# A hybrid attention kernel on one core: the first chunk of a layer, the head of a routing stage and the emptying of some row sums, rearranged

## The chip, the core and the metric

The kernel runs on one core of a Trainium2 chip. A core has a matrix engine (TensorE, PE in the profile; its weight loads are PEld), a vector engine (VectorE, DVE), a scalar engine (ScalarE, ACT), a general engine (GpSimd, POOL) and a sync engine (SyncE, SP) that mostly issues transfers. Every engine works through its own instructions in order and waits on semaphores for the others. The matrix engine writes to PSUM, which is handed out in banks of 128 x 512 values. The metric is the device time of one execution in microseconds (us). All data are float32.

## What is computed

The input is one image of 256 channels and 64 x 64 positions. Layer 0 is a windowed linear attention, layer 1 a softmax attention over all 4096 positions and a mixture of 8 experts, of which each position uses two:

```python
# layer 0: x + attention(groupnorm(x))
q, k = sigmoid(Wq x), sigmoid(Wk x);  v = Wv x / max(|Wv x|, 1e-12)      # 8 heads of 32 channels
for w in (1, 2, 4):                     # boxes of 64 // w around each position
    wk, wkv = box_sum(k), box_sum(outer(k, v))
    outs.append(q . wkv / (q . wk + 1e-6))
x = x + concat(outs) Wout + bout
# layer 1, t is the 4096 x 256 matrix of positions
q, k, v = split(layernorm(t) w_qkv + b_qkv)
t = t + softmax(q k^T / sqrt(256)) v w_out + b_out
xt = layernorm(t);  logits = xt Wr + br;  weights, idx = top2(softmax(logits))
y_e = gelu((layernorm(xt) * ln_g[e] + ln_b[e]) W1[e] + b1[e]) W2[e] + b2[e]   # for the two experts
t = t + sum(weights * y[idx])
```

## The kernel before

The positions are cut into 8 chunks of 512, or 32 tiles of 128. Instructions go into each engine's queue in the order in which the program makes them; a small planner (`behind`, `tick`, `flush`) defers the use of scores by a step or two, and `tc.issue_after` places an instruction behind a named one. There are four stages.

**Layer 0** works on two groups of four heads, one after the other. `prepare` (L309) forms k, v and their sums over cells of 64 positions, then q (`by_channel(0, i)`, L360, sigmoid L367) and, held in the list `later`, four calls that project k by channel. Then it computes the denominators: for each of the three windows it builds differences of running sums (`tall`, L490 to L499, the copy on ScalarE) and products with q (L514), and multiplies them by a small matrix on PE (L517). The calls in `later` are taken one by one after every product part of four rows (L528). `attend` (L590) then computes the attention without expanding the outer products: scores of q and k (L662 for the band's part, L734 for the chunk's), multiplied by masks on VectorE or, after a copy by ScalarE, on GpSimd (`masked`, L548 to L569, where lines 561 and 565 are), and multiplied by v into PSUM (L693, L750). For windows of 32 and 16 positions there are four bands; in each, two banks of row sums are begun from prepared cell sums (L681), filled (L693), and at the band's last step both are emptied by ScalarE into `raw` (L706, two copies per band; 2 windows x 4 bands x 2 groups make 32). Six banks hold scores, two hold sums. The output projection is L638, added to `t` at L642.

**Layer 1, projections** (L808 to L933). A prologue issues the weights' and biases' loads (L821 to L845), turns the bias rows by a PE transpose (L847) into columns (`bqk`, L849), forms the sums of the router's matrix and its product with the output weights (L856 to L882), and only then goes over the 8 chunks. For each chunk: statistics of the *next* chunk (`begin`, L793 to L799, with a square root on ScalarE), the reciprocal of this one's (L802), and for each of its four tiles a normalized tile `hn` on VectorE (L898, in a pool of two buffers), two transposes on PE (L808) and a copy by ScalarE (L809); then 16 products for q and k (L914; evicted by VectorE at L918, with the largest magnitude at L919) and 16 for v with the router's logits (L925; L932, L933).

**Layer 1, attention** (L970 to L1106) is one loop over query chunks, halves of the heads and key tiles. The denominators of a half are turned over through DRAM and applied some steps later, except for the very last one, where `divide` (L1069 to L1073) computes the reciprocal of a 128 x 512 bank at once and multiplies by it. After the loop, the last four tiles are projected (L972), added to `t` (L975), and their statistics taken (L793, L794).

**Routing and experts** (L1180 on). The routing's head loads three sets of the experts' rows, turns them into columns by three PE transposes (L1237 to L1240), stores them to DRAM (L1244), and computes the second normalization (L798 to L802, L1252 on), the logits (L1275 on) and the places of all positions. Then 36 expert steps follow (L1460 to L1496), whose columns are loaded back from DRAM, and the ending (L1537 on) combines the two experts' outputs.

## Time and profile before

| | us |
|---|---|
| median of 3 runs | 2881.29 |
| lowest and highest run | 2879.69, 2881.95 |
| the profiled execution | 2876.29 |
| its span (first to last instruction) | 2874.5 |
| layer 0, from the start to the last L638 | 0 to 1001 |
| layer 1's projections | 1001 to 1120 |
| layer 1's attention | 1120 to 2287 |
| routing, to the first expert product | 2287 to 2340 |
| experts and ending | 2340 to 2874.5 |

The mean clock granted to TensorE over the span is 0.976 of full speed. The profile's page gives busy times per engine, and the trace gives the start and length of every instruction with the idle time of its engine before it and what ended that. Where the releaser is called "issue", the engine waited for nothing that the trace shows. Times inside the execution are given below as the trace has them, in us from the start of the span.

### The profile page before, as it was taken

The page shows a single profiled execution, that of the slowest core. Times are in us where ns is not written, and L with a number is a line of the kernel's source. Part 1 is how long each engine was busy: PE and PEld are TensorE (multiplying, and loading weights), DVE is VectorE, ACT ScalarE, POOL GpSimd, SP SyncE. Part 2 cuts the span into 40 slices and gives each one's busy share as a digit, 9 for nine tenths or more (in the row PEclk, how much of TensorE's full clock was granted, in tenths as well). Part 3 has the DMA queues.
Part 4 walks back from the last instruction along what each step waited for, and adds up shares of the span by engine and source line. Part 5 has one row for each costly group of instructions (what it writes and reads, how often), then busy time and mean ns, then how long its engine had stood idle before and what let it go on. Part 6 is the DMA issues. An engine that isn't in the chain of part 4 may idle for free.

```text
span 2874.5 us, 73093 instructions
## 1 busy us (share of the span) xinstructions
PE 2722.7 (95%) x31182; PEld 1265.9 (44%) x31182; DVE 2078.1 (72%) x3019; ACT 1504.6 (52%) x2086; POOL 717.9 (25%) x804
## 2 busy tenths in 40 slices
PE   6889999988999999999999999999999779999996
PEld 5454346735434553222222222222222258888884
DVE  6758788575778777999999999999999841111113
ACT  3232423223332314888888888888888643222222
POOL 1067778116777621000000000000000022222220
PEclk9999999999999999999999999999999969999997
DMA  5000000000000000000000000000000056666665
GB/s 140 6 26 28 7 31 13 7 7 24 24 14 27 27 1 1 6 6 6 6 5 6 6 6 6 5 6 6 6 6 6 8 193 205 193 220 196 194 220 187
DMA packets 104212, 149.71 MB, mean 52 GB/s; under 512 B 18338, under 2 KB 79368, under 8 KB 103876
## 3 DMA queue, kind: packets, MB, share of 16 engines
q1 hardware_dynamic: 88984, 118.05, 12.7%
q0 software_dynamic: 6528, 17.83, 2.2%
q10 hardware_dynamic: 8364, 9.02, 0.9%
q8 instruction: 249, 4.08, 0.6%
q14 instruction: 87, 0.71, 0.1%
HBM read 126.76 MB, written 18.12 MB: 50 GB/s over the span
## 4 chain that ended last, share of the span: by engine, by line
PE 57%; DMA 2%; DVE 1%; issue 1%; ACT 0%; SPq 0%; POOL 0%; ACTq 0%; DVEq 0%; POOLq 0%
PE ps_two L1025 20%; PE ps_acc L991 18%; PE ps_hp L1485 8%; PE ps_yp L1494 8%; PE ps_den L972 1%; PE ps_den L991 1%; DMA y<-yrows 1%; PE ps_tp L1460 1%; DMA w<-in_L_ffn_W 0%; PE ps_two L972 0%; DVE t L1537 0%; DMA yrows<-y,target 0%; DVE rec L1072 0%; ACT pe L1036 0%; DVE total L1043 0%
## 5 line engine op out<-in xcount | busy, mean ns | idle before, releaser
L1036 ACT ACTIVATE pe<-ps_two 128x1024 f32<-128x1024 f32 x1024 | 992.4, 1021 | 142.5 <-PE ps_two L1025 127.3
L1043 DVE TENSOR_TENSOR total<-total,pe 128x1024 f32<-128x1024 f32 x928 | 1058.0, 1214 | 0.0
L1025 PE MATMUL ps_two<-qk 32*64 32x512 f32 x8192 | 620.2, 613 | 3.6 <-POOLq L978 1.8
L991 PE MATMUL ps_acc<-pe,v 128*32 128x512 f32 x4096 | 546.4, 605 | 0.2 <-ACT pe L1036 0.2
L561 ACT COPY sm<-ps_sc 128x384 f32<-128x384 f32 (+3 forms) x454 | 218.5, 511 | 523.8 <-PE ps_sc L734 344.3
L565 DVE TENSOR_TENSOR sm<-ps_sc,mask 128x512 f32<-128x512 f32 (+3 forms) x740 | 340.0, 519 | 71.8 <-PE ps_sc L734 68.0
L565 POOL TENSOR_TENSOR sm<-sm,mask 128x192 f32<-128x192 f32 (+3 forms) x428 | 350.1, 847 | 111.9 <-ACT sm L561 111.5
L1025 PEld LDWEIGHTS ps_two<-qk 32*64 32x64 f32 x8192 | 166.5, 129 | 421.0 <-PE ps_two L1025 379.0
L1488 ACT ACTIVATE hid<-ps_hp,cols 128x256 f32<-128x256 f32 (+1 forms) x288 | 133.0, 462 | 360.6 <-PE ps_hp L1485 359.5
L1303 POOL MEMSET on<- 128x256 f32 x1 | 0.3, 311 | 1166.6 <-PE ps_den L991 1166.6
L991 PEld LDWEIGHTS ps_acc<-pe,v 128*32 128x32 f32 x4096 | 80.7, 108 | 416.5 <-issue 402.5
L1485 PE MATMUL ps_hp<-xe,w 128*128 128x256 f32 (+1 forms) x1152 | 246.8, 371 | 0.0
L1494 PE MATMUL ps_yp<-w,hid 128*128 128x256 f32 x1088 | 240.8, 379 | 0.0
L734 PE MATMUL ps_sc<-qk 32*64 32x384 f32 (+3 forms) x3584 | 231.9, 458 | 0.0
L1485 PEld LDWEIGHTS ps_hp<-xe,w 128*128 128x128 f32 x1152 | 201.3, 190 | 39.5 <-ACT hid L1488 5.3
L1494 PEld LDWEIGHTS ps_yp<-w,hid 128*128 128x128 f32 x1088 | 204.2, 190 | 26.4
L750 PE MATMUL ps_acc<-sm,v 128*32 128x256 f32 (+3 forms) x2688 | 213.2, 419 | 0.2
L565 POOL TENSOR_TENSOR sm<-sm,ycut 128x384 f32<-128x384 f32 (+4 forms) x146 | 147.5, 1031 | 250.4 <-ACT sm L561 250.1
L1464 DVE TENSOR_SCALAR xe<-ps_tp,cols 128x256 f32<-128x256 f32 (+1 forms) x72 | 34.8, 525 | 239.6 <-PE ps_tp L1460 217.1
L565 DVE TENSOR_TENSOR sm<-ps_sc,ycut 128x384 f32<-128x384 f32 (+4 forms) x254 | 128.8, 559 | 90.0 <-PE ps_sc L662 88.0
L1496 DVE TENSOR_TENSOR y<-ps_yp,b 128x256 f32<-128x256 f32 x68 | 28.9, 424 | 194.8 <-PE ps_yp L1494 194.7
L734 PEld LDWEIGHTS ps_sc<-qk 32*64 32x64 f32 (+1 forms) x3584 | 108.6, 157 | 111.4 <-DVE sm L565 67.6
(237 smaller groups left out, 2230.6 us busy)
## 6 DMA issues: line engine op xcount, KB each, us to landing
w<-in_L_ffn_W SPq DMA_DIRECT2D x72, 1024.0 KB
by<-recs SPq DMA_DIRECT2D x48, 256.0 KB
b<-in_L_ffn_b SPq DMA_DIRECT2D x36, 128.0 KB
rows<-in_x SPq DMA_DIRECT2D x16, 256.0 KB
zrows<-act SPq DMA_DIRECT2D x4, 1024.0 KB
y<-yrows SPq DMA_DIRECT2D x8, 512.0 KB
y<-yrows ACTq DMA_DIRECT2D x8, 512.0 KB
rec<-recs SPq DMA_DIRECT2D x60, 64.0 KB
```

What stands on the lines that cost most here:

```text
L561: nc.scalar.copy(sm[:, :used], sc[:, :used])
L565: done = engine.tensor_mul(to, of, mk.unsqueeze(1).to_broadcast(list(to.shape)))
L734: nc.tensor.matmul(scs[h][u : u + rows, at : at + n], kT[hs[h], P * i + u : P * i + u + rows], qT[hs[h], CH * ix + CELL * c0 : CH * ix + C ...
L750: nc.tensor.matmul(acc[hs[h], CELL * c0 : CELL * c1], v[:, i, hs[h]], sms[h][:, at : at + n], start=not begun[0], stop=last and at == plac ...
L991: nc.tensor.matmul(to[D * hd : D * (hd + 1), :], lhsT(hd), rhs[:, hd, :], start=start, stop=stop, skip_group_check=True,)
L1025: nc.tensor.matmul(sc[hd // 2][CELL * u : CELL * (u + 1), hd % 2, :], qk[hs, 1, g, P * i + CELL * u : P * i + CELL * (u + 1)], qk[hs, 0, g ...
L1036: nc.scalar.activation(pe[:, pair, :], s, AF.Exp, scale=C**-0.5)
L1043: add = nc.vector.tensor_add(to, first[:, pair, :] if i == 1 else to, pe[:, pair, :])
L1464: nc.vector.tensor_scalar(xe[:, k, :n], tp[:, k, :n], cols[:, gain], cols[:, shift], op0=ALU.mult, op1=ALU.add,)
L1485: nc.tensor.matmul(hp[:, :n], w1[:, k, tok(m)], x_now[:, k, :n], start=k == 0, stop=k == KC - 1)
L1488: nc.scalar.activation(hid[:, m, :n], hp[:, :n], AF.Gelu, bias=cols[:, m : m + 1])
L1494: nc.tensor.matmul(yp, hid[:, m, tok(j)], w2[:, m, :], start=m == 0, stop=m == NH - 1)
```

## The change

It has seven parts.

- In layer 1's prologue the bias transposes and the router's products become two functions. Chunk 0's four normalized tiles and their transposes come first; then `biases()` and the statistics of chunk 1; then chunk 0's products; then `router()`, and then chunk 1. `issue_after` places them so on VectorE and on PE.
- The normalized tiles `hn` get four buffers instead of two.
- The experts' columns are turned right after chunk 2's products for v, with the rows loaded on SP and the copies on ScalarE; the store goes to SP too. They leave the routing.
- The last `divide` works in four quarters of 128 columns: reciprocal and product of each.
- The emptying of each band's two banks in layer 0 goes half to ScalarE and half to VectorE.
- The first deferred k projection is made before the denominators' loop starts, so each later one comes one part earlier.
- Square roots of a constant are placed where ScalarE's table of functions is to change: after the last sigmoid of layer 0's second preparation, and at the start of the routing stage.

```diff
+            if g == KC - 1:
+                with tc.issue_after(sigmoid[0]):
+                    nc.scalar.sqrt(root, ident[:, :1])
...
             q = qk[:, 0].rearrange("p (i n) -> p i n", n=CH)
+            later.pop(0)()
             for w, r in enumerate(REACH):
...
-                                    nc.scalar.copy(
+                                    (nc.vector.tensor_copy if u else nc.scalar.copy)(
                                         raw[:, :, q0 : q0 + CELL], accs[u].rearrange("p (i n) -> p i n", n=CELL)
                                     )
...
+    def expert_columns(pool, ps):
+        cols = pool.tile([P, NE, NH + 2 * KC], F32, name="cols")
+        at = 0
+        for name, n in (("L1_ffn_b1", NH), ("L1_ffn_ln_g", KC), ("L1_ffn_ln_b", KC)):
+            rw = pool.tile([NE * n, P], F32, name=f"{name}_rows")
+            nc.sync.dma_start(rw, a[name].rearrange("e (k p) -> (e k) p", p=P))
+            tp = ps.tile([P, CH], F32, tag="mm", name="ps_mm")
+            nc.tensor.transpose(tp[:, : NE * n], rw, ident[: NE * n, : NE * n])
+            nc.scalar.copy(cols[:, :, at : at + n], tp[:, : NE * n].rearrange("p (e k) -> p e k", e=NE))
+            at += n
+        nc.sync.dma_start(crows.rearrange("e p n -> p e n"), cols)
...
+            def biases():
+                tp = ps.tile([P, CH], F32, tag="mm", name="ps_mm")
+                nc.tensor.transpose(tp[:, :6], rows6, ident[:6, :6])
+                nc.vector.tensor_copy(bqk, tp[:, :6])
+
+            def router():
...
             begin(0)
             for c in range(NCH):
-                if c + 1 < NCH:
+                if 0 < c < NCH - 1:
                     begin(c + 1)
                 norm.end(NB * c, NB * (c + 1))
                 for i in range(NB * c, NB * (c + 1)):
-                    hn = work.tile([P, C], F32, name="hn")
-                    nc.vector.tensor_scalar(
+                    hn = work.tile([P, C], F32, name="hn", bufs=4)
+                    last = nc.vector.tensor_scalar(
...
+                if c == 0:
+                    with tc.issue_after(last.ins), tc.issue_after(turned.ins):
+                        biases()
+                        begin(1)
...
+                if c == 0:
+                    with tc.issue_after(biased.ins), tc.issue_after(product.ins):
+                        router()
+                if c == 2:
+                    expert_columns(win, ps)
...
                                     rec = work.tile([P, CH], F32, tag="rec", name="rec")
-                                    nc.vector.reciprocal(rec, den[0])
-                                    times(rec)
+                                    for n in range(CH // P):
+                                        nc.vector.reciprocal(rec[:, tok(n)], den[0][:, tok(n)])
+                                        nc.vector.tensor_mul(to[:, tok(n)], to[:, tok(n)], rec[:, tok(n)])
...
+        root = small.tile([1, 1], F32, name="root")
+        nc.scalar.sqrt(root, ident[:1, :1])
         cst.update(constants_of("m", wts))
...
-            cols = r_work.tile([P, NE, NH + 2 * KC], F32, name="cols", bufs=1)
...
-                nc.scalar.dma_start(rw, a[name].rearrange("e (k p) -> (e k) p", p=P))
...
-            nc.scalar.dma_start(crows.rearrange("e p n -> p e n"), cols)
```

The body of `router()` is the old prologue's, line for line, and is left out here.

## The prediction

> **What bounds the kernel now.** I read the page's first two parts, then the granted clock and the engines in windows of 1 us over the head of layer 1, then the timelines of that head, of a later chunk, and of the end of the attention, and the answer for line 706.

> ```profile
> PE 2722.7 (95%) x31182; PEld 1265.9 (44%) x31182; DVE 2078.1 (72%) x3019; ACT 1504.6 (52%) x2086; POOL 717.9 (25%) x804
> ...
> PEclk9999999999999999999999999999999969999997
> ```

> TensorE (PE) is busy for 95% of 2874.5 us, and its clock drops where it had nothing to do. None of the long loops behind that 95% (L991, L1025, L1485, L1494) changes, so only the gaps between them are in play. By windows (start:end, length, busy share of PE, PEld, DVE, ACT, POOL, then granted clock, DMA share, GB/s):

> ```profile
> 1003.00:1004.00 1.00, 0.00 (x0) 0.00 (x0) 1.00 (x7) 0.62 (x1) 0.00 (x0) 0.57 0.95 332
> ...
> 1019.00:1020.00 1.00, 1.00 (x2) 0.34 (x1) 1.00 (x5) 0.00 (x0) 0.00 (x0) 0.50 0.00 0
> 1020.00:1021.00 1.00, 1.00 (x4) 0.46 (x3) 0.41 (x2) 0.00 (x0) 0.00 (x0) 0.90 0.00 0
> ```

> PE stands still from 1000.6 to 1007.2 and then runs at half clock to about 1020, though its products have been dense since 1014.78. The timeline of that head (start, length, idle before with releaser):

> ```profile
> 1003.38 1.28 ACT L799 ACT_TABLE_LOAD   x1 [8.06 <-DVE ln_mv L794]
> ...
> 1007.26 0.24 PE L847 MATMUL ps_mm<-cst,bias_rows 6*128 6x6 f32 x1 [6.67 <-DMA L_attn_b_out_all<-in_L_attn_b_out]
> ...
> 1007.61 0.17 DVE L849 COPY bqk<-ps_mm 128x6 f32<-128x6 f32 x1 [2.95 <-PE ps_mm L847]
> ```

> PE starts on the bias rows at 1007.26. VectorE (DVE) stands 2.95 us before their eviction, with chunk 0's reciprocal and normalized tiles (first L898 at 1009.50) queued behind it; the first QKV product (L914) comes at 1014.78. A later chunk begins like this:

> ```profile
> 1054.93 0.73 PE L808 MATMUL ps_mm<-cst,hn 128*128 128x128 f32 x4 [0.49 <-DVE hn L898]
> ...
> 1056.13 4.13 PE L914 MATMUL ps_mm<-act,wqkv 128*128 128x512 f32 x9 [0.46 <-ACT act L809]
> ```

> Two short waits per chunk, one for a normalized tile, one for its copy. Who waits for L706's copies in layer 0 (us, times):

> ```profile
>   PEld ps_acc L681: 3.6, 6
>   PEld ps_acc L750: 2.8, 4
> ```

> 6.4 us is all that PE ever waits for them. And the end of the attention with the routing's head:

> ```profile
> 2277.91 3.36 DVE L1072 RECIPROCAL rec<-ps_den 128x512 f32<-128x512 f32 x1 [1.15 <-PE ps_den L991]
> ...
> 2282.11 3.80 PE L972 MATMUL ps_two<-wo,act 128*128 128x264 f32 x10 [2.72 <-DVE act L1067]
> ...
> 2289.93 0.17 DVE L1315 TENSOR_SCALAR steps<-cstm 128x16 f32<-128x16 f32 x1 [2.66 <-issue]
> 2292.52 0.31 DVE L1240 COPY cols<-ps_mm 128x64 f32<-128x64 f32 x2 [2.42 <-issue]
> ```

> Here DVE is the path: one reciprocal of 3.36 us holds PE, and 2.42 us pass ahead of the column copy that nothing in the profile explains, though PE had its input ready at 2288.2.

> **The change, part by part.** All of it is against the profiled execution, 2876.29 us.

> *Chunk 0 ahead of the router.* The new order on PE is transposes, bias transpose, chunk 0's products, its V products, and then the router's small products among chunk 1's transposes. On DVE, chunk 0's four tiles come before the bias eviction. With the root table loaded earlier (1.28 us off ACT's path), the tiles are made at about 1004 to 1006 and turned before the weights are in. The DMA share falls to 0.22 in 1006 to 1007 and the bias rows release PE at 1007.26. Adding their transpose, 0.24, the first product starts at 1007.5; it stands behind that landing on PE as the router did. The sixteen products took 1014.78 to 1024.43 = 9.65 with the first 5.3 us at half clock; I take the same, as in both orders they follow an idle stretch and small work: 1017.15. V products took 1024.43 to 1027.99 = 3.56: 1020.7. Router products were at half clock 1.02 + 1.00 + 1.09 + 0.60 + 1.07 = 4.8, so 2.4 at full: 1023.1. Their two evictions (0.43 each) stand between products: 0.8, 1023.9. Chunk 1's transposes took 1027.99 to 1030.42 = 2.43: 1026.3; the waits within them, 0.49 and 0.60, now hold router products: about 1025.3. Before, it was 1030.42. I take **-5.0**. Ends: the router at half clock throughout costs 2.4 more (-2.6); a start at 1006.9 and evictions fully covered gain 1.4 more (-6.5). Behind the moved bias eviction on DVE stand chunk 1's statistics (8 instructions, about 2.3 us) and then the evictions of chunk 0, whose first came 3.8 us after its products began, so they are covered; uncovered they would cost what DVE lacks, under 1 us.

> The row is that the clock was still 0.50 in 1019 to 1020, 5.3 us after dense products began and 12.7 after the first small one. [...]

> *Four normalized tiles instead of the pool's default.* At the six later boundaries the 0.49 goes; what is late next is ACT, whose copy (0.70 for two) holds L914 by 0.46 already. I take 0.35 x 6 = **-2.1**, ends 0 (ACT was as late) and -2.9 (6 x 0.49).

> *Expert columns in chunk 2.* Three transposes of 0.23 to 0.28 us each (rows L1239), with three copies by ACT: 0.75, and 0.25 for a bank that waits: **+1.0**, ends 0.4 (at full clock, no wait) and 2 (three waits of an ACT copy, 0.4, added). The transposes' rows are loaded some 40 us earlier. Those three loads join SP behind the weights, 0.37 to 0.46 each to issue; nothing is due on SP behind them, nor behind the column store, until 2274. Four DMA issues leave ACT's queue at the routing (0.53, 0.60, 0.33, 0.42), where ACT waited anyway.

> *Divide in quarters.* The reciprocal of 128x128 is 0.94 (row L620), a product of that size 0.29 (row L1319); in eight steps 4 x 1.23 = 4.9, less some 0.06 overlap per step: done at 2282.5 instead of 2282.05. But the first two quarters are done by 2280.3, and the last product's rows no longer come after ten products in a row (3.80, the clock going to 0.50). DVE's tail work from there is 2282.86 to 2287.27 = 4.41, of which 1.06 was waiting for PE; without it 2282.5 + 3.35 = 2285.9: **-1.35**, ends -0.5 (half of the 1.06 stays, the start as now) and -2.2.

> *Routing's head.* With no column copies the normalization's add (2292.75) stands directly behind L1315's step (2289.93). The two copies are 0.23; the 2.42 is either a code fetch behind a branch (the instruction queue's packets land at 2290.5 and 2293.0) or something the copies waited for. Either way the copies' place is gone, and the instructions behind the branch have shifted by eight. I take it as gone: **-2.65**, ends -0.2 (the gap stays, at the next instruction) and -2.8. The whole chain to the first expert product (2339.5) hangs on this DVE work, so it passes through. ACT's table load at 2288.51 had been hidden already: 0. What is late next is ACT's own chain (L1261, 15.8 us, ending 2312.26), which ends level with DVE's first piece but starts from the same root, so it moves too.

> *L706 split.* Sixteen of 32 copies, 0.589 each, leave ACT (9.4 us, at places where ACT waits) and come to DVE at 0.69 (the 128x512 copy, row L340). PE waits for the first copy of a pair, which stays. Behind DVE's copy stand the next step's masks. At 161.81 DVE is idle for 2.02 us, at 296.0 for 2.78, so 0.69 lies in that: **0**, ends -2 (a third of the 6.4) and +6.

> *k ahead of denominators.* The same PE instructions from 88.6 to 124.6; DVE's waits there (4.49 and 3.40) change places with them, and the long denominators to 138.87 are the same: **0**, ends -1 and +1. The square root's table load lands in layer 0's last preparation, where ACT waits 1.31 ahead of a copy at 612.82 needed at 617.94: 0.

> Sum: -5.0 - 2.1 + 1.0 - 1.35 - 2.65 = **-10.1**, so 2866.2 profiled. The median of the runs, 2881.29, stands 5.0 above the profiled execution; with that, **2871**.

> **The rivals.**
> *The head gives half (chance 0.2).* The 2.42 shows up again at the next instruction, and the router runs at half clock: 2.4 + 2.4 less. Net -5.3, time 2876. For it: PE's clock in this region took 13 us to rise, and the gap carries no releaser. Against it: the router now follows 13 us of dense products.

> *The copies on DVE hold the masks (chance 0.1), slower.* DVE works in order; if its copy waits for the sums as ACT did (5.7 us over 7 cases, 0.36 per copy) with the next masks behind, PE waits for their banks: 16 x (0.69 + 0.36) = +16.8, net +6.7, time 2888. It needs over 0.63 us of PE time per copy, so nearly all of it uncovered. For it: PE waits 67.6 us for DVE's masks at L734. Against it: idle times of 2 to 2.8 us at the places looked at, and 71.8 us of DVE waiting for PE before its masks.

> *The change does only the rest (inside the first).* If the tiles' order gave nothing at the later chunks and the columns cost 2 us, the sum would be -7.0: 2874.3.

> **How the numbers follow.** My forecast, 2871, has 0.7 with its own range of 2865 to 2876; the half gain 0.2; the slower case 0.1. 0.2% is 5.8 us, about what a measurement of this kernel can tell from no change: under 2875.5 is faster, over 2887.1 slower. Faster: 0.62 of the 0.7 and 0.08 of the half gain, 0.70. Slower: 0.08 of the 0.1. Same: the rest, 0.22. All best ends together give -17.0 (2864.3), all worst +5.7 (2887.0); the range goes 1 us of the runs' spread below the first, and ends at 2881, where the two faster cases and their bounds end, leaving out the slower one: 2863 to 2881.

> **What would show it.** The first QKV product at 1007 to 1008 and chunk 1's near 1025.4, with the clock at 1.00 by about 1013; later chunks 12.5 us apart, that of the columns a little longer; the last row statistic at about 2285.9 on the old scale; less than 1 us between L1315's step and the normalization's add; layer 0's end where it was, within 2 us. It would be wrong if layer 0 ends over 5 us later, if a new idle row of PE names the masks behind a DVE copy, or if the 2.4 us comes back as issue time on DVE.

## The result, and the profile after

The changed kernel took 2866.28 us (median of 6 runs, 2862.69 to 2871.48) against 2880.08 us (6 runs, 2879.19 to 2881.95): a ratio of 0.9951, 95% interval 0.9938 to 0.9964. Two further measurements on other chips gave 0.9956 (0.9942 to 0.9969) and 0.9955 (0.9941 to 0.9968). So it is faster, by 13 to 14 us where 10 were forecast, and 2866.3 lies just inside the forecast's own range (2865 to 2876).

The page after:

```profile
PE 2719.1 (95%) x31182; PEld 1264.0 (44%) x31182; DVE 2088.4 (73%) x3038; ACT 1497.5 (52%) x2075; POOL 717.9 (25%) x804
...
PEclk9999999999999999999999999999999979999997
```

ACT has lost 7 us and DVE gained 10, mostly the sixteen copies that changed hands; the long loops are the same. The page shows nothing of where the time went, so I cut the span into stages at the same instructions in every trace. Three executions of the changed program were profiled (two of them among the experiments below); each row begins where the one above it ends:

| stage, us | before | changed | again | third |
|---|---|---|---|---|
| layer 0, to the last L638 (after: L641) | 1000.59 | 1005.34 | 1000.67 | 999.61 |
| head: to the first product of chunk 1 | 29.83 | 23.28 | 23.34 | 23.47 |
| chunks 1 to 7 | 87.68 | 84.97 | 85.00 | 84.97 |
| to the last denominators of the attention | 1159.77 | 1159.71 | 1159.78 | 1159.70 |
| last divide, projection, statistics | 9.24 | 7.06 | 7.06 | 7.05 |
| branch to the normalization's add | 5.65 | 2.91 | 3.00 | 3.01 |
| rest of the routing | 46.78 | 47.48 | 47.09 | 46.91 |
| experts | 489.56 | 489.17 | 489.48 | 489.68 |
| ending | 45.41 | 44.62 | 44.51 | 44.67 |
| span | 2874.50 | 2864.56 | 2859.93 | 2859.10 |

The first two spans differ by 9.9 us, almost the forecast's 10.1, but that agreement is an accident: layer 0 happened to take 4.75 us longer in the first profile of the changed kernel, which the other two do not repeat, and the stages from layer 1 on gave 14.7.

The head, in the timeline after:

```profile
1008.05 0.20 ACT L807 ACTIVATE ln_rstd<-ln_rstd 128x4 f32<-128x4 f32 x1 [7.99 <-DVE ln_rstd L806]
...
1009.09 1.94 PE L816 MATMUL ps_mm<-cst,hn 128*128 128x128 f32 x8 [3.75 <-issue]
...
1011.86 0.24 PE L877 MATMUL ps_mm<-cst,bias_rows 6*128 6x6 f32 x1 [0.83 <-DMA bias_rows<-in_L_attn_b_qkv]
...
1012.03 8.91 PE L947 MATMUL ps_mm<-act,wqkv 128*128 128x512 f32 x16
```

No table load stands ahead of the square root, the transposes are done when the bias rows land, and the products follow at once: 6.7 us after layer 0 instead of 14.2. The granted clock is the column behind POOL's (1.00 is full speed). In steps of 3.4 us, the kernel before and then the changed one:

```profile
1010.00:1013.40 3.40, 3.31 (x16) 2.74 (x14) 2.00 (x6) 0.68 (x2) 2.17 (x3) 0.50 0.00 0
1013.40:1016.80 3.40, 2.76 (x6) 1.28 (x6) 2.82 (x14) 1.01 (x4) 2.24 (x3) 0.50 0.00 0
1016.80:1020.20 3.40, 3.40 (x6) 1.33 (x5) 1.60 (x5) 0.00 (x0) 0.00 (x0) 0.50 0.00 0
1020.20:1023.60 3.40, 3.40 (x10) 1.49 (x9) 2.62 (x8) 0.20 (x1) 0.00 (x0) 1.00 0.00 0
```

```profile
1008.80:1012.20 3.40, 2.28 (x10) 1.90 (x11) 2.76 (x11) 1.49 (x4) 0.00 (x0) 0.50 0.73 249
1012.20:1015.60 3.40, 3.40 (x4) 1.34 (x5) 3.40 (x16) 0.20 (x1) 3.11 (x5) 0.50 0.02 5
1015.60:1019.00 3.40, 3.40 (x9) 1.54 (x8) 3.40 (x6) 0.21 (x1) 2.67 (x4) 0.99 0.00 0
```

Before, a step with PE busy for 3.31 us of router products and transposes (1010.0 to 1013.4) was followed by two more at half clock, and the clock rose behind the first step that the 128x512 products filled (1016.8 to 1020.2). After, the first step of that kind (1012.2 to 1015.6) came at once.

A later chunk's start, after:

```profile
1039.16 1.28 PE L816 MATMUL ps_mm<-cst,hn 128*128 128x128 f32 x8
...
1040.90 7.13 PE L947 MATMUL ps_mm<-act,wqkv 128*128 128x512 f32 x16 [0.46 <-ACT act L817]
```

All eight transposes run without a wait for a tile; PE's wait for ScalarE's copy is 0.46 us, as before.

The end of the attention and the routing's head, after:

```profile
2273.39 1.77 DVE L1111 RECIPROCAL rec<-ps_den 128x128 f32<-128x128 f32 x2 [1.18 <-PE ps_den L1029]
...
2277.38 1.70 PE L1010 MATMUL ps_two<-wo,act 128*128 128x264 f32 x6 [0.86 <-DVE act L1112]
...
2283.21 0.18 DVE L1342 TENSOR_SCALAR steps<-cstm 128x16 f32<-128x16 f32 x1 [2.67 <-issue]
2283.29 0.17 DVE L806 TENSOR_SCALAR ln_rstd<-ln_mv 128x32 f32<-128x32 f32 x1
```

PE waits 0.5 and 0.9 us for quarters of the divide where it waited 2.72 for all of it, and the 2.42 us behind the first instruction of the routing are gone.

### The profile page after: what moved, and what is told of

It reads as the page before. It is cut to its first block, busy times and chain, and to the rows that moved or that the text cites. A ratio compares the mean times of both kernels' runs of the same rounds, so it can differ in the third digit from the quotient of the medians.

```text
span 2864.6 us, 73084 instructions
## 1 busy us (share of the span) xinstructions
PE 2719.1 (95%) x31182; PEld 1264.0 (44%) x31182; DVE 2088.4 (73%) x3038; ACT 1497.5 (52%) x2075; POOL 717.9 (25%) x804
```

## The experiments

The theory to test: the head, the buffers, the divide and the place behind the branch give the gain, each in its stage; layer 0 gives nothing. The rivals: the 2.42 us were a wait of the column copies; router products warm the clock as well as any; layer 0's 4.75 us belong to the change. Some kernels ran once, and are read by their stages; a single time is given, but it can't tell 2 us from nothing here.

**Three parts undone in one kernel**, each in a stage of its own.

```diff
-                                    (nc.vector.tensor_copy if u else nc.scalar.copy)(
+                                    nc.scalar.copy(
...
-                    hn = work.tile([P, C], F32, name="hn", bufs=4)
+                    hn = work.tile([P, C], F32, name="hn")
...
+                                    nc.vector.reciprocal(rec, den[0])
+                                    nc.vector.tensor_mul(to, to, rec)
```

> The changed kernel with three parts undone that lie in different stages: both copies of a band on ScalarE, two buffers for the normalized tiles, the last divide at once. Read by stage against the changed kernel. Chunks: my account is that each of the six later boundaries gets 0.55 us longer (3.3 in all); if the buffers were not what shortened them, 0. Divide: the last statistics come 2.2 us later after the end of the attention. Bands: between -1 and +1 us for all of layer 0. Routing's head: vector-engine code is the same there as in the changed kernel, with no column copies, but the first instruction behind the branch stands eight places earlier, where it stood in the kernel before. If the 2.42 us was code loading, it comes back between the first instruction and the next (over 2 us); if it was a wait of the column copies, the next instruction follows within 0.2 us. Time with code loading about 2874, without about 2872.

Four of the six later boundaries went from 12.27 back to 12.82 us, one from 12.27 to 12.93, and the one with the columns from 12.93 to 13.43; the divide's stage from 7.06 to 9.06. Layer 0 ended at 997.7, sooner than in any profile of the changed kernel, so no loss by the copies on ScalarE is seen. And the gap came back, at the same distance behind the branch, though no column copy stands there:

```profile
2282.59 0.18 DVE L1341 TENSOR_SCALAR steps<-cstm 128x16 f32<-128x16 f32 x1 [2.93 <-issue]
2282.67 0.18 DVE L806 TENSOR_SCALAR ln_rstd<-ln_mv 128x32 f32<-128x32 f32 x1
...
2285.11 0.42 DVE L1301 TENSOR_TENSOR logit<-ln_mv,wr_sum 128x256 f32<-128x256 f32 x1 [2.27 <-issue]
```

Two instructions run, then 2.27 us pass. In the kernel before two had run as well, the step at 2289.93 and a wait. A packet of 8 KB of the instruction queue starts at 2280.8, the next at 2283.4; each is followed by instructions 1.7 to 1.8 us later. One time: 2868.76, against 2872.97 for the kernel before on the same chip.

**The columns back in the routing's head**, copied by VectorE as before, all else as changed.

```diff
-                if c == 2:
-                    expert_columns(win, ps)
...
+            cols = r_work.tile([P, NE, NH + 2 * KC], F32, name="cols", bufs=1)
...
+                nc.vector.tensor_copy(
```

> The changed kernel with the experts' columns back in the routing's head, as before (row loads on ScalarE's queue, copies on VectorE), and out of chunk 2. Chunk 2 to 3 gets about 0.65 us shorter. In the routing's head the code-loading theory expects the copies to cost 0.3 us and no gap over 1 us ahead of them, as the first instruction behind the branch is six places later than in the kernel before: net about -0.3 us. The rival, a wait of these copies, expects the 2.4 us ahead of them again: net about +2.1 us.

```profile
2282.51 0.17 DVE L1353 TENSOR_SCALAR steps<-cstm 128x16 f32<-128x16 f32 x1 [2.67 <-issue]
2282.93 0.31 DVE L1278 COPY cols<-ps_mm 128x64 f32<-128x64 f32 x2 [0.25 <-issue]
2283.15 0.17 DVE L806 TENSOR_SCALAR ln_rstd<-ln_mv 128x32 f32<-128x32 f32 x1
```

The copies are there and the gap is not: the first instruction lies six places behind where it lay before. They cost 0.57 us between the first instruction and the add, rather than 0.3. Chunk 2 to chunk 3 fell from 12.93 to 12.28. One time: 2866.0.

**Eight more tiny instructions in the kernel before.**

```diff
+                spare8 = work.tile([P, 1], F32, name="spare8")
+                for _ in range(8):
+                    nc.vector.memset(spare8, 0.0)
```

> The kernel before with eight more tiny fills of one scratch column on VectorE at the start of layer 1's attention, nothing else changed; the column copies stay in the routing's head. Code loading: the first instruction behind the branch moves by eight places, and the 2.42 us ahead of the column copies falls under 0.5 us; routing ends 2.4 us earlier. A wait of the copies: the 2.42 us stays as it is. The fills themselves lie beside PE's attention: 0.

```profile
2288.14 0.18 DVE L1318 TENSOR_SCALAR steps<-cstm 128x16 f32<-128x16 f32 x1 [2.67 <-issue]
2288.53 0.31 DVE L1243 COPY cols<-ps_mm 128x64 f32<-128x64 f32 x2 [0.22 <-issue]
```

From the first instruction to the add 0.62 us instead of 2.82. VectorE's records ahead of the branch's target are 4570 in the trace of the kernel before and 4569 with three parts undone, the two with the gap; they are 4578 here, 4577 in the changed kernel and 4576 with the columns back, and none of these has it (counts to within a record or two). With the two runs above this settles that the 2.42 us were no wait of the copies: the gap goes with the place of the branch's target. That it is code loaded in pieces, and that the target's place in a piece decides, is my reading; the trace doesn't show which packet holds which instruction. In the changed kernel, too, a second packet starts 2.4 us behind the first (2281.4 and 2283.8), but no gap follows there. The column copies were only the next instructions there. One time: 2872.84, no better than the 2872.97 of the kernel before: in its profile the attention took 1.5 us longer, with a step at half clock at its start.

**The router ahead of chunk 0's products again.**

```diff
                         biases()
+                        router()
                         begin(1)
...
-                if c == 0:
-                    with tc.issue_after(biased.ins), tc.issue_after(product.ins):
-                        router()
```

> The changed kernel with the router's small products put back ahead of chunk 0's products (behind its transposes and the bias transpose), all else as changed. If small products and transposes do not raise the clock: they run at half clock, 4.8 us and their evictions; the clock rises one or two steps of 3.4 us after the dense products begin, as in the changed kernel; chunk 1 then starts 2.5 to 3.5 us later than in the changed kernel. The rival, that any work on PE warms the clock: it is up when chunk 0 begins, the sixteen products take 7 instead of 8.75 us, and chunk 1 starts within 1 us of where it does in the changed kernel.

Head to chunk 1: 25.49 us, 2.0 to 2.2 more than as changed, just under my 2.5. One time: 2868.15. The clock was at 0.50 from 1007.6 to 1017.8: 6.5 us of router work from 1008.4 to 1014.9, with two of chunk 0's passes among it, did not raise it; it rose 2.9 us after the uninterrupted products began:

```profile
1008.41 1.02 PE L886 MATMUL ps_mm<-wqkv,ones 128*128 128x8 f32 x4
...
1014.92 7.68 PE L948 MATMUL ps_mm<-act,wqkv 128*128 128x512 f32 x14
```

The rival (within 1 us) is out.

**No early square root, and the k projections one part later.**

```diff
-            if g == KC - 1:
-                with tc.issue_after(sigmoid[0]):
-                    nc.scalar.sqrt(root, ident[:, :1])
...
-            later.pop(0)()
```

> The changed kernel with two parts undone in different stages: no square root of a constant in layer 0's second preparation, so that the function table is loaded in layer 1's head; and the k projections again one part behind the denominators. Head: the table load, 1.28 us, stands on the path to the normalized tiles again; chunk 0's products waited for the bias rows 0.4 us after the last copy, so they start 0.7 to 1.3 us later than in the changed kernel; if the early load was worth nothing they start at the same time. Denominators: my account is that the order of k projections is worth under 0.3 us at the end of either preparation (the first scores come at the same time after the first k projection, apart from steps of the clock); the rival is 1 us or more.

```profile
1002.94 1.28 ACT L802 ACT_TABLE_LOAD   x1 [7.90 <-DVE ln_mv L797]
...
1007.67 4.72 PE L942 MATMUL ps_mm<-act,wqkv 128*128 128x512 f32 x6 [0.26 <-ACT act L812]
```

The products start 7.36 us after layer 0, 0.7 to 1.0 later than in the three profiles of the changed kernel; now ACT's last copy releases them, not the bias rows. The k projections: against the second profile of the changed kernel this one is 1.97 us behind ahead of them, 3.17 within them, and 1.87 at the first scores. The order gives 1.2 us on the way and nothing at the end, where this kernel is 0.1 nearer. One time: 2861.68, against 2862.2 for the changed kernel on that chip.

**Spare products to keep the clock up.** Seven, three, and three with the columns moved; the control is the changed kernel itself.

```diff
             begin(0)
+            idle = ps.tile([P, CH], F32, tag="mm", name="ps_mm")
+            for _ in range(7):
+                nc.tensor.matmul(idle, ident, act[:, 0, chunk(NCH - 1)], start=True, stop=True)
```

> The changed kernel with seven products of 128x512 into a bank that nobody reads, put on PE ahead of chunk 0's transposes, where PE stood idle for about 4 us. If the clock falls because PE is idle for a step of 3.4 us, it stays up or is down for less: chunk 0's products take about 7 us instead of 8.75, and chunk 1 starts 1.5 to 2 us sooner after the end of layer 0. The rival, that the clock in this place follows something else (or that the extra products delay the transposes): chunk 1 starts at the same time or up to 1 us later. Against the kernel before, -15 by the first and -13 by the second.

```profile
1003.06 6.28 PE L922 MATMUL ps_mm<-act,cst 128*128 128x512 f32 x14 [0.79 <-DVE t L645]
...
1010.85 7.13 PE L950 MATMUL ps_mm<-act,wqkv 128*128 128x512 f32 x16 [0.48 <-ACT act L817]
```

Chunk 0's products took 7 us, at full clock, as the first theory has it; but each spare product is two passes, the fourteen ended at 1009.3, when the first tile had been there since 1005.9, and chunk 1 started 0.8 to 0.9 us later than as changed. The clock then dropped once more, at 1025.1, after a step of router products and transposes, and the next chunk took 13.28. Time 2867.66 (2864.58 to 2870.92), 0.9968 of before (0.9956 to 0.9980): a loss against the changed kernel on that chip, 2862.2. The head and that chunk explain 1.9 of these 5.5 us; the rest is open.

> As the kernel with seven products in the head, and with both copies of each band in layer 0 on ScalarE again. If the half on VectorE is worth nothing, as I have it, it is equal to the other within 1.5 us; if it was a gain of several us, slower by that; if it holds up the masks (the rival of the prediction), faster by 1 to 3 us, all of it in the bands.

Its edit is the seven products and `nc.scalar.copy` for both halves. 2868.2 (2865.89 to 2870.45), ratio 0.9970 (0.9958 to 0.9982), against 2867.66 for its twin: the half on VectorE shows no worth either way, though the runs of each spread over 4.6 to 6.3 us. The two groups' attention took 372.1 + 370.1 us here and 372.3 + 369.0 there.

> The changed kernel once more, as a second profile of the same program and for times on the same chip as the two others. My account: the same code moves by 2 to 4 us from one execution to the next, at the steps of the clock near 60 to 80 us and in the first bands (140 to 215 us); so layer 0 should end 2 us or more away from where it ended in the first profile (1005.4), while the chunks of 12.27 us, the 2.0 to 2.2 us of the divide and the 0.1 us behind the branch stay. If layer 0 ends at 1005 again, its 4.75 us are the change's own.

2862.2 (2861.36 to 2868.54). Layer 0 ended at 1000.7, not 1005.3, and the other stages are those of the first profile (table above):

```profile
1000.71 0.69 DVE L645 TENSOR_TENSOR t<-ps_sc,t 128x512 f32<-128x512 f32 x1 [0.17 <-PE ps_sc L641]
```

So the 4.75 us were not the change's.

With `range(3)` in place of `range(7)`:

> The changed kernel with three spare products instead of the seven of the earlier run (six passes of 0.43 us, 2.6 us, over before the normalized tiles are there). If seven were right in kind and only too long: chunk 0's products start 6.4 to 6.9 us after layer 0 as in the changed kernel, the clock stays up, and chunk 1 starts 1.2 to 1.6 us sooner than in the changed kernel. If 2.6 us of work do not keep the clock up, chunk 1 starts where it does in the changed kernel.

Now chunk 0 starts 6.33 us after layer 0 and chunk 1 at 21.12, 2.2 to 2.4 us sooner than as changed, more than expected. But the time is 2862.72 (2861.35 to 2865.45), ratio 0.9956 (0.9943 to 0.9970): no better than its control, the changed kernel on the same chip, 2861.31. In the profiled execution the stage behind took the gain back: from the first scores to the last denominators 1161.30 us against 1157.75. Steps of the clock at the change from the chunks to the attention, in this kernel:

```profile
1107.90:1111.30 3.40, 1.54 (x24) 0.71 (x26) 1.47 (x5) 0.28 (x2) 0.00 (x0) 1.00 0.00 0
1111.30:1114.70 3.40, 2.33 (x19) 0.30 (x8) 0.00 (x0) 3.10 (x3) 0.00 (x0) 0.50 0.00 0
```

and in the control:

```profile
1106.30:1109.70 3.40, 1.91 (x11) 1.26 (x9) 2.62 (x11) 0.66 (x4) 0.00 (x0) 1.00 0.00 0
1109.70:1113.10 3.40, 1.95 (x24) 0.63 (x24) 0.00 (x0) 1.69 (x2) 0.00 (x0) 1.00 0.00 0
1113.10:1116.50 3.40, 2.73 (x32) 0.59 (x32) 0.76 (x1) 3.37 (x4) 0.00 (x0) 1.00 0.00 0
```

PE waits for the first scores' release for 1.86 us here and 1.83 in the control, and a second time behind them (1.07 and 1.79). In this kernel the first wait fell into one step, PE was busy for 1.54 of 3.4 and the clock went to half for three steps; in the control the waits were spread so that PE was busy for 1.91 and 1.95, and the clock stayed at 1.00.

> The changed kernel a third time, as the control of the other two on the same chip and for the spread between executions. Its stages from layer 1 on are as in its first two profiles within 0.5 us (head to chunk 1 23.3, chunks 12.27, divide and projection 7.06, 0.1 behind the branch's first instruction); the stretch up to the first scores and the first group's attention differ by up to 2.5 us each.

2861.31 (2860.68 to 2865.25); every stage from layer 1 on within 0.5 us, as expected.

> As the kernel with three spare products, and the experts' columns back in the routing's head, but copied by ScalarE and with their transfers on SP, so that nothing of them stands on VectorE. If their cost in chunk 2 is only the place on PE and ScalarE: chunk 2 to chunk 3 falls from 12.93 to 12.27, the routing stays as long as in the changed kernel within 0.3 us, net -0.65. If ScalarE's copies hold up the square root there: routing longer by 0.5 to 1 us, net about 0.

Its further edit is the columns in the routing with `nc.scalar.copy` and `nc.sync.dma_start`. Chunk 2 to chunk 3 fell from 13.15 to 12.54 and the routing kept its length (46.91): -0.6, as expected. 2861.22 (2857.27 to 2863.29), ratio 0.9949 (0.9936 to 0.9963); its attention too had a step of half clock, 1160.34.

**The exponential's table early.** On top of the last kernel:

```diff
+                early = work.tile([1, 1], F32, name="early")
+                nc.scalar.activation(early, ident[:1, :1], AF.Exp)
                 done = []
```

> As the kernel with three spare products and the columns copied by ScalarE, and one exponential of a single value at the very start of layer 1's attention, so that the table of the exponential (1.28 us, now loaded after the first scores are there, with PE idle for 1.8 us behind it) is loaded while PE makes the first scores. The stretch from the first scores to the last denominators takes 1157.75 in the changed kernel when the clock is up; it should take 1156.4 to 1156.8. The steps of the clock between the chunks and the attention (2.6 to 3.6 us in five of twelve profiles) should come less often, as the idle time there falls from 3.7 to 2.5 us; one profile can't settle how often. Against the kernel before: -14 to -18 us. If the load was hidden already: 1157.75 and no change.

```profile
1110.92 1.28 ACT L1046 ACT_TABLE_LOAD   x1 [1.20 <-POOLq L1017]
1111.01 2.00 PE L1066 MATMUL ps_two<-qk 32*64 32x512 f32 x24 [1.83 <-POOLq L1017]
```

The load now runs beside the first scores, and PE's second wait there is 0.36 us instead of 1.69 in the last kernel. The attention took 1159.30 with two steps of half clock, 1.04 less than the last kernel's with two; without them it was not seen, so the 1156.4 to 1156.8 stay untested. 2863.0 (2861.85 to 2864.36) against 2881.79 on that chip, a ratio of 0.9936 (0.9922 to 0.9950): the lowest ratio of all, though its interval overlaps the changed kernel's.

## Why the prediction was right, and where it was not

The direction, the stages and most mechanisms held; three terms were too small, one too large, and one was right for a reason that I had left open. The stages gave 4.6 us more than the sum, and part of that is chance: two of the terms depend on when the clock changed in the one profile of the kernel before.

- *Head, -5.0; measured -6.5.* The start was right (6.9 us after layer 0 forecast, 6.4 to 6.7 measured). The step that failed is "The sixteen products took 1014.78 to 1024.43 = 9.65 with the first 5.3 us at half clock; I take the same": counted alike they took 8.75, 9.09 and 9.28 in the three profiles of the changed kernel. I had taken the 5.3 us as fixed, but full clock came 3.6, 4.3 and 4.7 us after the first product in these profiles, 5.4 in the kernel before, 5.7 with the columns back: in the windows of 3.4 us above it came behind the first that these products filled (1016.8 to 1020.2 and 1012.2 to 1015.6), and where the steps of 3.41 us lie differs between executions. So part of the -6.5 is chance: with eight more fills, whose head is that of the kernel before, the head took 28.88 and not 29.83, and against it the gain is 5.4 to 5.6, near the forecast. The rest, from the V products' end to chunk 1, took 4.3 instead of 4.7. Router work ahead of these products did not raise the clock: 6.5 us of it, in the run with the router first, left it at 0.50.
- *Four tiles, -2.1; measured -3.3* (0.55 at four of the six boundaries, against 0.35). The discount for ScalarE failed: "what is late next is ACT" had me take 0.35 of the 0.49. PE's wait for ACT's copy is 0.46 before and after, so all of the 0.49 goes, and 0.06 more because the eight transposes run in one go (1.28 us against 0.60 and 0.73). That is beyond the bound that I gave (-2.9), which was that one wait's length.
- *Columns, +1.0; measured +0.65.* No bank waited.
- *Divide, -1.35; measured -2.2, of which 2.0 come back when it is undone.* The mechanism is right. The quarters were sized from a product row of 0.29 and a reciprocal of 0.94; pairs took 0.42 and 1.77. But a good 1 us of the gain hangs on the clock. With the divide at once, the stage took 9.24 and 9.06 us where the clock fell 5.3 to 5.5 us after the last denominators, into the projection, and 8.06 in the run with eight more fills, where it fell after 10 (ten products in 2.49 us and not 3.80, and the wait of 1.06 is gone). In quarters it took 7.04 to 7.07 in all eleven profiles. So the gain is 1.0 or 2.2, and the two profiles that I compared had the dear case.
- *Routing's head, -2.65; measured -2.74.* I named code loading and a wait of the copies as the two readings. It was no wait of the copies, and code loading agrees with all five traces; the gain is a matter of eight instruction places, and an edit ahead of the branch can bring the gap back, as the first experiment did.
- *L706 split and k ahead, 0 and 0.* Nothing is seen of either: 2868.2 and 2867.66 in the pair of runs, 0.1 us in the trace. The slower rival (the masks held by the copies, 2888) is out; PE's wait for VectorE's masks at the line of L734 is 66.0 us after the change, against 67.6.
- *The 5.0 us added for the profiled execution.* One execution of the changed kernel differs from another by up to 5.7 us in layer 0 alone (999.61 to 1005.34 in three profiles), so such a term stands for chance. For the changed kernel it was nothing (2866.34 profiled, 2866.28 median): that 2871 was 4.7 too high is this term, and that the 2866.2 forecast for the profiled execution was met is the accident of layer 0.

## What to carry to other kernels

Cut two traces into stages at the same instructions before believing that a sum of terms was right: here a span difference of 9.9 us agreed with 10.1 while the parts were -14.7 and +4.75. Take a second profile of the kernel before as well, and ask of every stage whether the clock changed in it. The gap with no releaser behind a branch (2.42 us before, 2.27 with three parts undone) came and went with the place of the code; shift such code by a few instructions and take another profile before crediting an edit with it. And a few us of PE idle time can cost twice, once as idle and once as half clock: waits of 1.86 and 1.07 us were followed by three steps at 0.50, waits of 1.83 and 1.79, spread over two steps, by none. So a gain ahead of such a place can be taken back behind it, as with three spare products.

## What was not expected of the hardware

**Steps nearly as busy ended differently.** One of those 4 is the drop at 1025.1 in the kernel with seven spare products: that step held router products of 8 columns and transposes alone, with PE busy for 0.79 of it. In the three kernels with three spare products a step of such work alone was busy for 0.84 to 0.85 and kept the clock. At half clock, a step busy for 3.32 of 3.41 us with such work was followed by half clock again in the kernel before (1010.0 to 1013.4) and with eight more fills. So were four steps that L1432's products (128x144, bf16) filled in the changed kernel's first profile (2305.9 to 2319.5, at 0.50); why, no run shows.

**The same code took different times at such places.** The change from the chunks to the attention holds PE's two waits, 1.8 us each at full clock. In 6 of the 14 profiles the clock fell there (once two steps behind), and from its first scores the attention took 1159.3 to 1161.5 us instead of 1157.8 to 1158.2. The three kernels with three spare products are among the six; whether that is chance is not known. Near 70 us the changed kernel's first profile had 6.8 us at half clock and its second 3.4, and the first scores came at 143.3 and 140.7. The remaining difference of these two, 2.3 us in the first group's attention, fell in its first bands (140 to 215 us) with the clock up; its cause is open.
